# A hybrid of state-space scans, additive attention and graph-routed experts: later PSUM evictions, a softplus step through PSUM, another share of lists and gathers beside the attention, and another order of the last quarters

## The chip, the cores and the metric

The kernel runs on one core of one Trainium2 chip, in one launch. The core has five engines, each with a queue of its own that runs in order: TensorE (PE, with its weight loads as PEld), VectorE (DVE), ScalarE (ACT), GpSimd (POOL) and SyncE (SP, which issues most DMAs). The metric is the device time of one execution in microseconds. Fourteen runs of the kernel before took 15459.08 to 15480.63, with a median of 15470.4.

## The reference, cut to what matters

All data is float32: x is 4 x 32 x 96 x 256, four batches of 3072 tokens with 256 channels.

```python
xn = group_norm(x)
x = x + mamba_d(mamba_t(xn))            # two selective scans, along 96 steps, then along 32
t = x.reshape(4, 3072, 256)
# additive attention, U = 32
q, k = ln(t) @ Wt, ln(t) @ Wx
e = (tanh(q[:, :, None] + k[:, None] + bh) * Wa).sum(-1) + ba
t = t + softmax(e) @ ln(t)
# graph attention over 1048576 edges gives gates; 4 experts, top 2
h = ln(t) @ W_gat                        # 12288 rows
agg = segment_softmax_sum(h, edges)      # scores, exp, sums by destination
w = softmax(top2(mean_heads(ln(agg))))
t = t + sum_e w_e * (gelu(ln(t) @ W1[e] + b1[e]) @ W2[e] + b2[e])
```

Inside a scan block the step size is a softplus, `dt = softplus(dt_w @ dbl + dt_b)`, the state is `h = exp(dt * A) * h + dt * B * u`, and `y = sum(h * C)`. Both ends of the 1048576 edges are drawn from 65536 numbers, while there are 12288 rows: an edge with a destination outside drops out, and a source outside reads the last row. The kernel sorts the edges out itself; those with a source outside are only counted per destination.

## The kernel before, in words

**Order of the work.** For PE, ACT, DVE and POOL the instructions stand in the order in which the program writes them. Two generators are interleaved by hand. `Attention.units` (L779) yields twice per slot: a slot is one column of the attention, that is one tanh over 128 x 3072 on ScalarE (L802, with three buffers `th`). After each yield the other generator, `steps`, adds one half slot of other work. The kernel runs through these stages: the scans of the first batch alone; attention of batches 0 to 2 beside the scans of the next ones; the last attention beside edge lists, early expert products and gathers; and the tail.

**Attention.** Eight slots make a unit of 32 queries, and there are 384 units. In the first half of a slot the tanh is issued, then the other work's first half, then 16 products that reduce the tanh of two slots before into the bank `pe` (L778; one buffer). After the eighth, VectorE takes the maximum of `pe` (L848) and ScalarE the exponential `pr` (L855). The steps that follow are done one per slot, in its second half: four transposes of `pr` on PE into the bank `ptw` and their copy to `pT` on VectorE (`turn`, L862 and L864), two more with their copy, 24 products with the values (L871), and the copy of their sum (L877). All of these use one PSUM buffer in turn (`psum`, one bank). Four units make a tile of 128 queries; its last steps (`tile_tail`: L900 to L937) go on in the same way: the maxima `mx`, a transpose `pm` and its reduction `g`, a second transpose and `f`, an exponential, four small products `sf` on GpSimd (L921), the products `po` with them (L926), and the output with its statistics and its store. A step that returns nothing lets a piece of side work (`beside`) follow in that slot: normalization and keys of the next batch, tables of finished tiles.

**Scans.** `Layer0.run` gives a block of 384 columns 48 slots. `back` fills them with decays on ScalarE (L378, into two PSUM tiles dA), inputs dB (L386), scans (L395, two of 384 columns at a time) on VectorE and products and sums on GpSimd (L402 to L411). `front` prepares the next block in the same slots: at slots 33 to 44 the softplus. For each of four chunks a product fills the bank `pt` (L284), VectorE forms the rectified part and an argument in SBUF (L300, L301), ScalarE takes exp in place (L308), GpSimd adds one (L312), VectorE takes the rounding error of that sum (L316), GpSimd subtracts it (L320); then one Ln over all four (L329), and two additions (L335). These slots are fixed by hand. The first 17 blocks are "lead" blocks with another sharing between the engines. `Beside` uses the bank `ex` of the pool `ps_x` in slots 0 to 30 for some expert products.

**Lists, counts and gathers.** Once the scans are done, `steps` gives each slot `EDGE_US` = 1.9 units of list work (`Edges.sort`, VectorE, each piece with its own estimate in us). The lists end with one-hot products that count edges (L1174, L1188), one pair per slot, as far as PE has room by the planner's account. When the lists have ended, 324 destination gathers (`gd`, L1009, GpSimd) are issued, three per slot. In PE's room `Experts.early` also computes expert units in pairs.

**Tail.** `tail` lays its work out on numbered steps; an expert unit (block of 512 rows, expert) takes three. 37 units are left. The edges come in four quarters of nine parts of 12 columns; part m stands at step `t = G0 + PART * m // 2`: gathers of its rows (L1286, and the destination gathers not done yet) ten steps ahead, scores at t, one-hots (`spread`, L1319 and L1323) and products (`place`, L1333) after. A quarter's `finish` computes the gates of its six blocks. Blocks whose expert outputs are there before their gates are "kept": stored to memory (L1669), fetched again (L1724, four outputs in one transfer) and summed with the gates at steps four apart (L1662). The quarters' order is

```python
QUARTERS = 3, 2, 0, 1
for m in range(4 * PQ):
    j = QUARTERS[m // PQ] * PQ + m % PQ
    t = G0 + PART * m // 2
```

Of the kernel before, what the change touches and what calls it, by code (L numbers as in the profile page):

```python
# [17 lines left out]
F32 = mybir.dt.float32  # L18
# [8 lines left out]
P = 128  # L27
# [34 lines left out]
EDGE_US = 1.9  # L62
G0, PART = 10, 6
QUARTERS = 3, 2, 0, 1
# [10 lines left out]
class Layer0:  # L75
# [96 lines left out]
    def front(self, blk, lead):  # L172
# [107 lines left out]
        def step(e, s_mm, s_out):  # L280
            @at(s_mm)
            def _():
                v["pt"] = ps.tile([P, T], F32, tag="pp", name="pt")
                nc.tensor.matmul(v["pt"], self.wf["dt"][:, e * P:(e + 1) * P], v["dbl"][:DR, :],  # L284
                                 start=True, stop=True)

            ua, ub, dt = (lambda: v["ua"][:, e, :]), (lambda: v["ub"][:, e, :]), (
                lambda: blk["dt"][:, e, :])  # L290

            @at(s_out)
            def _():
                bias = self.wf["dtb"][:, e:e + 1]
                if lead:
                    nc.scalar.activation(dt(), v["pt"], AF.Relu, bias=bias)
                    nc.scalar.activation(ua(), v["pt"], AF.Abs, bias=bias)
                else:

                    nc.vector.tensor_scalar(dt(), v["pt"], bias, 0.0, ALU.add, ALU.max)  # L300
                    nc.vector.scalar_tensor_tensor(ua(), dt(), -2.0, v["pt"], ALU.mult, ALU.add)  # L301

            @at(s_out + 1)
            def _():
                if lead:
                    nc.scalar.activation(ua(), ua(), AF.Exp, scale=-1.0)
                else:
                    nc.scalar.activation(ua(), ua(), AF.Exp, bias=self.wf["dtb"][:, e:e + 1])  # L308

            @at(s_out + 2)  # L310
            def _():
                nc.gpsimd.tensor_scalar(ub(), ua(), 1.0, None, ALU.add)  # L312

            @at(s_out + 3)
            def _():
                nc.vector.scalar_tensor_tensor(ua(), ub(), 1.0, ua(), ALU.subtract, ALU.subtract)  # L316

            @at(s_out + 5)
            def _():
                nc.gpsimd.tensor_tensor(dt(), dt(), ua(), ALU.subtract)  # L320

        step(0, 33, 33)
        step(1, 34, 35)
        step(2, 36, 36)
        step(3, 37, 37)

        @at(41)
# [3 lines left out]
        for e in range(0, EC, 2):  # L331
            @at(44 + e // 2)
# [14 lines left out]
    def back(self, blk, then):  # L347
# [121 lines left out]
        for e in range(EC):  # L469
# [19 lines left out]
            put(12 * e + 4, gate_product(e), 0 if blk["lead"] else 1)  # L489
            put(12 * e + 5, gate_tanh(e))  # L490
            put(12 * e + 6, gate_out(e))
# [140 lines left out]
class Attention:  # L632
# [40 lines left out]

    def psum(self, name):
# [91 lines left out]
    def units(self, side):  # L766
# [24 lines left out]
        while i < B * PER + LAG or todo:  # L791
            b, col = self.entry, self.col = divmod(i, PER)
            if b < B and "krep" not in self.state[b]:

                yield
                yield
# [7 lines left out]
            yield  # L804
            busy = tail = None
# [11 lines left out]
            if tail:  # L817
# [3 lines left out]
                todo = tail()  # L821
            elif todo:
                busy = todo.pop(0)()
# [14 lines left out]
    def unit_tail(self, b, n, pe):  # L838
# [20 lines left out]
        def turn(i0, i1):  # L859
            pt, pr, pT = self.psum("ptw"), v["pr"], v["pT"]  # L860
            for i in range(i0, i1):
                nc.tensor.transpose(pt[:, (i - i0) * P:(i - i0 + 1) * P], pr[:, i * P:(i + 1) * P],  # L862
                                    self.ident)
            nc.vector.tensor_copy(pT[:, i0:i1, :].rearrange("p i x -> p (i x)"),  # L864
                                  pt[:, :(i1 - i0) * P])

        def values():
# [5 lines left out]
            s["pv"] = pv  # L873
            return "pv"

        def kept():
            nc.vector.tensor_copy(pvs[:, u, :], s["pv"][:, :C + 1])  # L877

        first, second = (lambda: turn(0, 4)), (lambda: turn(4, NK))
        first.us, second.us, values.us = 0.7, 0.4, 2.9  # L880
        steps = [first, second, values, kept]
        if u == NU - 1:
            first, *rest = self.tile_tail(b, t, nb, pvs)
            steps = steps[:3] + [lambda: (kept(), first())[1]] + rest
        return weights

    def tile_tail(self, b, t, nb, pvs):
# [10 lines left out]
        def factors():  # L898
            nc.sync.dma_start(x, src)
            nc.vector.tensor_scalar(mx, nb, -1.0, self.ba, ALU.mult, ALU.add)  # L900
            g = self.wk.tile([NU, QU], F32, tag="g", name="g")
# [3 lines left out]
            nc.vector.tensor_reduce(g, pm[:NU, :P].rearrange("p (q r) -> p r q", q=NQT), AX.X,  # L905
                                    ALU.max)
            nc.vector.tensor_copy(g4, g.unsqueeze(1).to_broadcast([NU, NQT, QU]))
            s["g4"] = g4

        def factors2():  # L910
# [3 lines left out]
            nc.vector.tensor_tensor(f, mx, pf[:, :NU], ALU.subtract)  # L914
# [8 lines left out]
        def together():  # L923
# [4 lines left out]
            s["po"] = po  # L928
            return "po"

        def outputs():
            po = s["po"]
# [6 lines left out]
        return [factors, factors2, factors3, spread, together, outputs]  # L939
# [260 lines left out]
class Graph:  # L1200
# [4 lines left out]
    def __init__(self, ctx, tc, a, ed, tab_s, tab_a, gates):  # L1205
# [8 lines left out]
        self.got, self.parts = {}, 4 * CQ // GP  # L1214
# [65 lines left out]
    def gather(self, j):  # L1280
# [4 lines left out]
        for u in range(GP):  # L1285
# [3 lines left out]
            ed.gather(q, c0 + u)  # L1289
        self.got[j] = gs  # L1290

    def scores(self, j):
# [13 lines left out]
        self.v = v  # L1306

    def spread(self, j, g):
# [13 lines left out]
        v = self.v[:, g * GG:(g + 1) * GG, :]  # L1322
# [4 lines left out]
    def place(self, j, g, ol, rh):  # L1327
        nc = self.nc
        c0 = (j * GP + g * GG) % CQ
        if c0 == 0:  # L1330
            self.pa = self.ps.tile([P, JB], F32, tag="pa", name="pa")
        for u in range(GG):
            nc.tensor.matmul(self.pa[:, :NT * ROW], ol[:, u, :],  # L1333
# [3 lines left out]
    def finish(self, q):  # L1337
# [5 lines left out]
        nc.vector.tensor_tensor(acc, acc, self.pa[:, :NT * ROW].rearrange("p (n f) -> p n f", f=ROW),  # L1343
# [331 lines left out]
def tail(tc, a, ed, ex, w, tab_s, tab_a, gates):  # L1675


    with ExitStack() as ctx:
# [14 lines left out]
        for m in range(4 * PQ):  # L1693
            j = QUARTERS[m // PQ] * PQ + m % PQ
# [9 lines left out]
            if m % PQ == PQ - 1:  # L1704
                fin, q = {}, QUARTERS[m // PQ]
# [157 lines left out]
def whole(tc, a, dram, out):  # L1863
# [11 lines left out]
    with ExitStack() as ctx:  # L1875
        actx, lctx, ectx = ExitStack(), ExitStack(), ExitStack()
        with tc.manual_schedule(engines={E.PE, E.Activation, E.DVE, E.Pool}):
# [10 lines left out]
            def steps():  # L1888
# [15 lines left out]
                while True:  # L1904
# [23 lines left out]
                    for _ in range(3 if columns else 0):  # L1928
# [102 lines left out]
```

## Time and profile before

| what | us or share |
|---|---|
| median of 14 runs | 15470.4 |
| the profiled execution, its own time | 15481.81 |
| its span, first to last instruction | 15479.8 |
| ACT busy | 12181.3 (79%) |
| PE busy | 11839.5 (76%) |
| DVE busy | 11078.3 (72%) |
| POOL busy | 8983.7 (58%) |
| tanh of the attention, L802, 3072 of 2.847 | 8666.6 |
| granted TensorE clock, mean | 0.882 |

The profile is one execution. Its page gives each engine's busy share in 40 slices of 387 us, a digit per slice in tenths; "waits" name who waited, at which line, for whom, with total us, times and the longest; groups by line give count, busy us, mean ns, and the idle time just before with what ended it; a timeline gives start and duration. A DMA_INDIRECT on POOL is a gather; L802 means line 802 of the kernel before. Idle time of an engine that does not set the pace costs nothing.

### The profile page before, as it was taken

What the parts mean: (1) busy time and instruction counts of PE and PEld (TensorE: products, weight loads), DVE (VectorE), ACT (ScalarE), POOL (GpSimd) and SP (SyncE); (2) the same over time, 40 slices, a digit from 0 to 9 for tenths busy, and PEclk for the clock granted to TensorE, in tenths of its full rate; (3) what the DMA queues carried; (4) which work ended last, traced back from release to release, by engine and by line L of the source; (5) the groups of instructions that cost most, each with busy time, mean ns of one, the idle gap of its engine ahead of it and who ended that gap; (6) DMA issues with size and microseconds to landing.
All of it is one profiled execution on the core that took longest, in us unless ns stands there. A gap on an engine that the chain in (4) does not pass through costs nothing.

```text
span 15479.8 us, 224265 instructions
## 1 busy us (share of the span) xinstructions
PE 11839.5 (76%) x86496; PEld 5198.1 (34%) x86496; DVE 11078.3 (72%) x15711; ACT 12181.3 (79%) x9326; POOL 8983.7 (58%) x6586
## 2 busy tenths in 40 slices
PE   5666665777777777888888777788877878887897
PEld 2223332222222233333333333333333334443454
DVE  7888888777777787777777877577767783331368
ACT  3444334999999979999999899999998989998221
POOL 4555557777777767777777677577750000007663
PEclk8988886888888878889898888999988989998998
DMA  5666665445444444454444444355541000001224
GB/s 190 206 203 203 196 201 162 144 147 152 148 147 147 151 156 145 148 152 150 147 145 154 153 145 151 112 155 152 151 129 40 23 16 15 10 25 22 52 62 127
DMA packets 1197833, 1986.89 MB, mean 128 GB/s; under 512 B 411984, under 2 KB 645072, under 8 KB 1194320
## 3 DMA queue, kind: packets, MB, share of 16 engines
q1 hardware_dynamic: 1169104, 1967.10, 40.7%
q0 software_dynamic: 27648, 5.36, 0.9%
q8 instruction: 680, 11.14, 0.3%
q14 instruction: 401, 3.28, 0.1%
HBM read 1864.71 MB, written 107.35 MB: 127 GB/s over the span
## 4 chain that ended last, share of the span: by engine, by line
ACT 18%; PE 17%; DVE 9%; POOL 6%; issue 6%; DMA 1%; SPq 0%; DVEq 0%; POOLq 0%; ACTq 0%
ACT th L802 13%; PE pe L778 6%; POOL gd L1009 2%; ACT dA L378 2%; PE pv L871 2%; DVE h L395 2%; PE po L1585 2%; PE pa L1333 2%; PE ph L1577 1%; POOL h L402 1%; ACT pr L855 1%; PE ptw L862 1%; POOL gs L1286 1%; PE ex L1502 1%; DVE dB L386 1%
## 5 line engine op out<-in xcount | busy, mean ns | idle before, releaser
L802 ACT ACTIVATE th<-krep,qsel 128x3072 f32<-128x3072 f32 x3072 | 8666.6, 2847 | 403.5 <-PE pe L778 385.6
L778 PE MATMUL pe<-th,wa_blk 128*32 128x384 f32 x49152 | 5110.4, 544 | 1637.7 <-ACT pr L855 1261.3
L402 POOL TENSOR_TENSOR h<-h,bC 128x768 f32<-128x768 f32 x2048 | 3782.0, 1847 | 2872.5 <-DVE h L395 2636.5
L395 DVE TENSOR_TENSOR_SCAN h<-dA,dB 128x384 f32<-128x384 f32 x4096 | 3681.9, 940 | 818.4 <-ACT dA L378 614.3
L778 PEld LDWEIGHTS pe<-th,wa_blk 128*32 128x32 f32 x49152 | 1472.0, 117 | 4272.8 <-issue 1946.0
L386 DVE TENSOR_TENSOR dB<-bB,dtu 128x768 f32<-128x768 f32 x2048 | 1945.2, 950 | 133.3 <-DMA bB<-bc 89.7
L378 ACT ACTIVATE dA<-dt,t_A 128x380 f32<-128x380 f32 x2048 | 1134.4, 572 | 993.3 <-DVE h L395 987.6
L378 ACT ACTIVATE dA<-dt,d_A 128x372 f32<-128x372 f32 x2048 | 1108.7, 563 | 674.5 <-DVE h L395 667.9
L421 PE MATMUL py<-h,ident 128*128 128x384 f32 x2176 | 990.8, 587 | 693.9 <-POOL h L402 693.0
L921 POOL TENSOR_SCALAR sf<-sel,f 128x32 f32<-128x32 f32 x384 | 153.4, 423 | 2316.3 <-ACT f L917 2196.3
L409 POOL TENSOR_TENSOR h<-h 128x768 f32<-128x768 f32 x752 | 1424.5, 1894 | 46.9
L864 DVE COPY pT<-ptw 128x512 f32<-128x512 f32 (+1 forms) x768 | 425.5, 554 | 1120.5 <-PE ptw L862 1119.5
L871 PE MATMUL pv<-xn,pT 128*32 128x257 f32 x18432 | 1092.4, 385 | 84.3 <-DVE pT L864 82.6
L421 PEld LDWEIGHTS py<-h,ident 128*128 128x128 f32 x2176 | 437.2, 219 | 1252.3 <-POOL h L402 1028.2
L410 POOL TENSOR_TENSOR h<-h 128x384 f32<-128x384 f32 x752 | 798.2, 1061 | 58.9
L411 POOL TENSOR_TENSOR y<-y,h 128x384 f32<-128x384 f32 x752 | 767.7, 1021 | 59.0
L871 PEld LDWEIGHTS pv<-xn,pT 128*32 128x32 f32 x18432 | 585.4, 111 | 633.7 <-DVE pT L864 147.6
L1286 POOL DMA_INDIRECT gs<-tab_s,si x432 | 504.6, 1168 | 265.4 <-issue 122.1
L316 DVE SCALAR_TENSOR_TENSOR uab<-uab 128x384 f32<-128x384 f32 x256 | 390.8, 1527 | 194.3 <-POOL uab L312 190.1
L1659 ACT ACTIVATE h<-ph,b 128x512 f32<-128x512 f32 x148 | 100.4, 687 | 533.5 <-PE ph L1577 533.2
L1009 POOL DMA_INDIRECT gd<-tab_a,di x432 | 428.2, 991 | 133.1 <-issue 133.1
L848 DVE TENSOR_REDUCE nb<-pe 128x1 f32<-128x768 f32 x384 | 361.8, 942 | 196.4 <-PE pe L778 196.2
(292 smaller groups left out, 15395.1 us busy)
## 6 DMA issues: line engine op xcount, KB each, us to landing
bB<-bc SPq DMA_DIRECT2D x2048, 384.0 KB
bC<-bc SPq DMA_DIRECT2D x2048, 384.0 KB
all<-kept SPq DMA_DIRECT2D x19, 2048.0 KB
x<-x SPq DMA_DIRECT2D x144, 256.0 KB
x<-x SPq DMA_DIRECT2D x192, 128.0 KB
xt<-xn2T SPq DMA_DIRECT2D x41, 512.0 KB
kept<-ko SPq DMA_DIRECT2D x39, 512.0 KB
qsel<-xn2T SPq DMA_DIRECT2D x75, 256.0 KB
```

The costliest lines, as they stand in the source:

```text
L378: nc.scalar.activation(inner(dA[:, :T]), inner(blk["dt"][:, e, :]), AF.Exp, scale=blk["w"]["A"][:, e, i + s:i + s + 1])
L386: nc.vector.tensor_tensor(dB, blk["bB"].pop(j), z["dtu"].unsqueeze(1).to_broadcast([P, SB, T]), ALU.mult)
L395: nc.vector.tensor_tensor_scan(h[:, s, :], z.pop(("dA", e, i + s))[:, :T], z["dB"][:, s, :], 0.0, ALU.mult, ALU.add)
L402: nc.gpsimd.tensor_tensor(h, h, blk["bC"].pop(j), ALU.mult)
L409: nc.gpsimd.tensor_tensor(h0, h0, h1, ALU.add)
L410: nc.gpsimd.tensor_tensor(h0[:, 0, :], h0[:, 0, :], h0[:, 1, :], ALU.add)
L411: nc.gpsimd.tensor_tensor(y[e], y[e], h0[:, 0, :], ALU.add)
L421: nc.tensor.matmul(z["py"], self.ident, h[:, s, :], start=(i == 0), stop=(i == DS - 1))
L778: nc.tensor.matmul(pe[q * QU:(q + 1) * QU, j, :KQ // 2], self.wa[:, k, :], th[:, c0:c0 + KQ // 2], start=(k == 0), stop=(k == NK - 1))
L802: nc.scalar.activation(th, s["krep"], AF.Tanh, bias=s["qsel"][:, col:col + 1])
L871: nc.tensor.matmul(pv[q * QU:(q + 1) * QU, :C + 1], pT[:, i, q * QU:(q + 1) * QU], s["xn"][:, q * NK + i, :], start=(i == 0), stop=(i == N ...
L1009: self.nc.gpsimd.indirect_dma_start(out=self.gd[:, q, c, :], out_offset=None, in_=self.tab_a[q].rearrange("p n f -> (p n) f"), in_offset=b ...
```

## The change

Constants: `EDGE_US` 1.9 becomes 2.4, `PART` 6 becomes 5, and `QUARTERS` goes: the quarters come in the order 0, 1, 2, 3. Destination gathers beside the attention: two per slot instead of three. In the tail, each part of quarters 0 to 2 also issues four destination gathers of quarter 3. So that quarters can overlap, `v` and `pa` are kept by part and quarter.

The softplus of blocks that aren't lead: exp goes to the bank `ex`, VectorE does the addition (before: GpSimd) and the subtraction from that bank in one slot, and the four chunks stand two slots apart. GpSimd's subtraction, Ln and the two additions follow; the gate product of the last chunk moves one slot.

The attention: evictions of the small bank are put on a list, `later`, which is worked off in the first half of the next slot, after the other generator's half and before the scores. A tile's first step is split (maxima, then factors), and side work goes ahead of a step instead of after it.

```diff
-EDGE_US = 1.9
-G0, PART = 10, 6
-QUARTERS = 3, 2, 0, 1
+EDGE_US = 2.4
+G0, PART = 10, 5
...
                 else:
-                    nc.scalar.activation(ua(), ua(), AF.Exp, bias=self.wf["dtb"][:, e:e + 1])
+                    v["u"] = self.ps_x.tile([P, 512], F32, tag="ex", name="u")[:, :T]
+                    nc.scalar.activation(v["u"], ua(), AF.Exp, bias=self.wf["dtb"][:, e:e + 1])
...
             @at(s_out + 2)
             def _():
-                nc.gpsimd.tensor_scalar(ub(), ua(), 1.0, None, ALU.add)
-
-            @at(s_out + 3)
-            def _():
-                nc.vector.scalar_tensor_tensor(ua(), ub(), 1.0, ua(), ALU.subtract, ALU.subtract)
-
-            @at(s_out + 5)
+                if lead:
+                    nc.gpsimd.tensor_scalar(ub(), ua(), 1.0, None, ALU.add)
+                else:
+                    nc.vector.tensor_scalar(ub(), v["u"], 1.0, None, ALU.add)
+                    nc.vector.scalar_tensor_tensor(ua(), ub(), 1.0, v["u"], ALU.subtract,
+                                                   ALU.subtract)
...
+            @at(s_out + (5 if lead else 3))
             def _():
                 nc.gpsimd.tensor_tensor(dt(), dt(), ua(), ALU.subtract)
 
-        step(0, 33, 33)
-        step(1, 34, 35)
-        step(2, 36, 36)
-        step(3, 37, 37)
-
-        @at(41)
+        for e, (s_mm, s_out) in enumerate(((33, 33), (34, 35), (36, 36), (37, 37)) if lead else
+                                          ((33, 34), (35, 36), (37, 38), (39, 40))):
+            step(e, s_mm, s_out)
+
+        @at(41 if lead else 43)
...
-            @at(44 + e // 2)
+            @at(44 + e // 2 * (1 if lead else 2))
...
+            g = 12 * e + (5 if e == EC - 1 and not blk["lead"] else 4)
+            put(g, gate_product(e), 0 if blk["lead"] else 1)
+            put(g + 1, gate_tanh(e))
+            put(g + 2, gate_out(e))
...
             yield
+            late, self.later = self.later, []
+            for f in late:
+                f()
             busy = tail = None
...
+            elif todo and hasattr(todo[0], "us"):
+                if not todo[0].full:
+                    beside()
+                todo.pop(0)()
+                busy = True
             elif todo:
-                busy = todo.pop(0)()
+                todo.pop(0)()
...
-            nc.vector.tensor_copy(pT[:, i0:i1, :].rearrange("p i x -> p (i x)"),
-                                  pt[:, :(i1 - i0) * P])
+            self.later.append(lambda: nc.vector.tensor_copy(
+                pT[:, i0:i1, :].rearrange("p i x -> p (i x)"), pt[:, :(i1 - i0) * P]))
...
-            s["pv"] = pv
-            return "pv"
-
-        def kept():
-            nc.vector.tensor_copy(pvs[:, u, :], s["pv"][:, :C + 1])
+            self.later.append(lambda: nc.vector.tensor_copy(pvs[:, u, :], pv[:, :C + 1]))
+
+        steps = [self.step(lambda: turn(0, 4), 0.7), self.step(lambda: turn(4, NK), 0.4),
+                 self.step(values, 2.9, True)]
...
+        for c in range(4 * j, min(4 * j + 4, CQ)):
+            ed.gather(3, c)
...
-            j = QUARTERS[m // PQ] * PQ + m % PQ
+            j = m
...
-                    for _ in range(3 if columns else 0):
+                    for _ in range(2 if columns else 0):
                         ed.gather(*columns.pop(0))
```

The rest of the diff does the same for the tile's last steps: the reduction `g`, the factors `f` and the output with its statistics and store are put on `later`, and the step with the maxima and the load of x stands by itself, put on `later` by the last unit's value products.

## The prediction

> **What bounds the kernel now.** I read the page's 40 slices for the stages, then the busy time by stage, then the waits of ScalarE in each.
>
> ```profile
> PE   5666665777777777888888777788877878887897
> DVE  7888888777777787777777877577767783331368
> ACT  3444334999999979999999899999998989998221
> POOL 4555557777777767777777677577750000007663
> ```
>
> ```profile
> core 0: us, PE busy (x) PEld busy (x) DVE busy (x) ACT busy (x) POOL busy (x), PEclk, DMA share, GB/s
> 2570.00:11533.00 8963.00, 7005.69 (x57369) 2895.90 (x57368) 6794.42 (x9265) 8448.32 (x6290) 6520.75 (x4668) 0.88 0.48 147
> 11533.00:12747.00 1214.00, 920.53 (x8466) 388.56 (x8470) 933.66 (x1490) 1023.57 (x423) 27.80 (x41) 0.89 0.10 31
> 12747.00:13920.00 1173.00, 1037.14 (x11196) 494.48 (x11192) 450.70 (x889) 1142.94 (x469) 24.25 (x57) 0.94 0.04 13
> 13920.00:14350.00 430.00, 325.38 (x2984) 142.26 (x2977) 71.05 (x139) 356.42 (x149) 307.96 (x332) 0.87 0.17 28
> 14350.00:15480.00 1130.00, 945.02 (x2904) 548.78 (x2902) 675.34 (x1237) 228.66 (x285) 626.92 (x546) 0.91 0.32 82
> ```
>
> The rows are the stages: attention beside the scans, lists, one-hot counts, gathers, tail (the scans alone, before 2570, keep their code). ScalarE, with its tanh of 2.85 us per slot, sets the pace until 14350: 94% busy in the first row, 97% in the third. So up to there a gain is a ScalarE wait that goes. In the tail it is PE, 84% busy.
>
> **Beside the scans (2570 to 11856).** ScalarE's waits here, the most this stage can give:
>
> ```profile
> ACT dA L378 <- DVE h L395: 305.5, 355, 7.4
> ACT th L802 <- PE pe L778: 218.1, 212, 5.6
> ACT pr L855 <- DVE nb L848: 55.2, 48, 13.7
> ```
>
> VectorE waits far longer (633.1 us for ptw at L864, 152.1 for pt at L300), but only what reaches ScalarE counts. For each gap of over 0.3 us before a dA I looked, in the trace, for VectorE's longest stall from 5 us before the gap on: 40.6 us of gaps stand behind uab L316, 27.9 behind dt L300, 22.2 behind g L905, 73 behind qsel, hb and xTc (not changed), 84.8 behind a busy VectorE, 0.3 behind the pT copy. So the long ptw wait is mostly slack, and deferring that copy gives almost nothing here.
>
> ```profile
> L316 DVE SCALAR_TENSOR_TENSOR uab<-uab 128x384 f32<-128x384 f32 x180 | 295.6, 1643 | 94.0 <-POOL uab L312 89.8
> L301 DVE SCALAR_TENSOR_TENSOR uab<-dt,pt 128x384 f32<-128x384 f32 x180 | 99.7, 554 | 6.2
> ```
>
> The same operation takes 1.64 us with both inputs in SBUF beside GpSimd's work, 0.55 us with one in PSUM. After, VectorE does the addition (like L300, 0.61 us) and the subtraction (like L301, 0.55): 1.16 for 1.64, times 184: 88 us less, and GpSimd loses 184 x 1.24 us. The steps now start in slots 34, 36, 38, 40, one PSUM bank each in turn, so the waits for pt and for GpSimd's sum go. I count the three named gaps (91 us) and half of the busy ones (42). The exp into PSUM I price like dA (0.56 for 0.60 us, 6 us in all): nothing. Its bank, ex, is free from slot 31 on, and each exp comes a slot after the subtraction that empties the bank; one that waited would hold the tanh behind it. The sums of dt (L335) end in slot 46 and the last gate in 43; they are read from slot 48 on, so the two slots more are covered. The eight added table loads are in the tail, where ScalarE is idle.
>
> [...]
>
> What it adds: each eviction now stands behind the next slot's scans (two of 0.94 us). The second pT copy starts 4.2 to 4.9 us (medians by batch) into a slot of 3.7 to 4.1, some 0.3 to 0.8 into the next one; behind the scans it ends near 2.5. The value products wait for it. They start at 2.1 to 2.9 now and take 2.8; the scores queued behind them on PE end at 2.7 to 3.7 of their slot, and the tanh after needs their buffer by 3.7 to 4.1. I take 0.1 us for each of 277 units, 30 us; the ends are nothing and 0.9 us (250), the room that the fastest of these batches has. Behind a late tanh all of ScalarE's queue is late, the decays too. Sum: -91 - 42 + 30, about **-100**; ends -220 (all busy gaps and a fifth of the waits for pe go too) and +120 (0.9 us per unit).
>
> The tile's own last steps (L900 to L935) each move by half a slot; the load of x and the store to x2 go with them on SP. That store waits there for x (873 us in all, 61 times), with loads of bB and bC queued behind, for which VectorE waits 89.7 us; store and x move together, so the wait is no longer: nothing. PE's wait of pm for mx (87.5 us) goes; that is in the gaps behind g.
>
> **Lists.** By the starts of the tanh, 346 slots take 1233 us (3.56 each).
>
> ```profile
> ACT th L802 <- PE pe L778: 119.3, 91, 8.1
> ACT pr L855 <- DVE nb L848: 69.1, 20, 13.7
> ```
>
> VectorE is busy 934 us of 1214 and waits for most of the rest, so it is full. A slot takes 2.4 units of lists for 1.9: laying the program out gives 274 slots, then 72 more at the counting stage's 2.99 us. VectorE's work left in the 274 is 934 less 72 slots of attention at 0.31 and two expert pairs at 8.7 (eight L1616, four L1628), 895 us or 3.27 a slot; that is the lower end, with all its waits gone. The upper is today's slot with 0.5 us more, 4.07. I take 3.6, near today's row: 274 x 3.6 + 72 x 2.99 + two pairs' gelu (13) = 1214: **-20** (-110 to +110).
>
> **Counting.** Both orders have about 385 slots at 2.99, with 28 us of ScalarE waits. The deferred copies stand behind a one-hot that itself waits for PE (L1174, 177.8 us): **+10** (-28 to +40).
>
> **Gathers beside attention.**
>
> ```profile
> L1009 POOL DMA_INDIRECT gd<-tab_a,di x320 | 303.9, 950 | 97.1 <-issue 97.1
> ```
>
> Each costs 0.95 + 0.30 = 1.25 us, so three per slot are 3.76 us: 108 slots take 397 us, 3.68 each, GpSimd's pace. It reaches ScalarE through sf: PE's waits for sf are 58.9 us in three places, up to 23.0, and th then waits 71.4. At two per slot GpSimd needs 2.5 us, under the 2.99, over 162 slots that end at slot 737 of 768. The last 118 slots fall from 435 us to 118 x 3.05 (2.99, and the gelu of two expert pairs, as today): **-75** (-50 to -90).
>
> **Tail.** Both orders have 37 expert units of three steps. From the timeline a unit is 16 products of 0.43 us and 32 of 0.226 on PE, 14.1 us; a part's placing is 24 of 0.403, 9.7 us. Before: a part each three steps, 23.8 us, and the trace has 23 to 24 late on; but the first nine parts (quarter 3, 24 gathers each) come 30 us apart (14472 to 14742), on GpSimd. After: 2.5 steps, 11.75 + 9.7 = 21.4 us on PE; 16 gathers at 1.45 (24 took 35) are 23.2. GpSimd starts at 14390 and the first placing is at 14472, its first 16 gathers are done by about 14415, so it has some 50 us in hand, and loses 27 x 1.8 = 49. So PE leads: 14472 + 35 x 21.4 = 15221, three gate computations inside the stretch at 12 us (36 for 23.5 in the trace), 15257, and 14 steps of units alone at 4.7: 15323. What follows:
>
> ```profile
> 15398.14 0.65 DVE L1343 TENSOR_TENSOR acc<-acc,pa 128x480 f32<-128x480 f32 x1
> ...
> 15417.95 0.26 DVE L1402 TENSOR_TENSOR gates<-gates,tot 128x96 f32<-128x96 f32 x1
> 15418.24 15.76 DVE L1662 SCALAR_TENSOR_TENSOR y<-all,gates,y 128x256 f32<-128x256 f32 x32
> ```
>
> Now the last quarter's gates (20 us) and six blocks' sums (62 us to the end) follow PE's last product. After, quarter 3's gates are ready at step 107, beside the units; the six blocks remain: 15385. **-95** (-120 to 0). Twenty more stores and five more fetches on SP, 20 MB, hide under DMA queues that are 32% busy; without that cover, at the 184 GB/s of the last 140 us, 110 us.
>
> [...]
>
> **The sum.** -100 - 20 + 10 - 75 - 95 = -280. The profiled execution took 15481.8 (span 15479.8); the median is 15470.4, 11.4 less. 15481.8 - 280 - 11.4 = **15190**.
>
> **Rivals.** (1) Beside the scans the freed gaps only become others: ScalarE waits for PE and VectorE in turn at each unit's end. For it: the ptw waits are mostly slack. Against: L316's stall has a price of its own. -180: 15290. (2) The tail doesn't do what it says: GpSimd at 1.5 us a gather and the added 20 MB hold PE, and 95 is lost: 15285. (3) Slower: a deferred copy holds the value products, the scores behind them miss their slot, and the tanh waits once per unit, 277 + 98 times. It decides from 280 / 375 = 0.75 us each; at 1.2 us it is +450 - 280: 15640. For it: PE is 83% busy there, and the scores end within 1 us of their limit. Against: PE has slack later in each unit.
>
> **Chances.** Forecast 0.62, (1) 0.18, (2) 0.08, (3) 0.12. A measurement of this kernel can tell about 0.2%, 31 us, from no change. From the first three 0.03, from (3) 0.02 fall within that: faster 0.85, same 0.05, slower 0.10. The range, 15040 to 15410, takes in the first three with the scan stage's two ends, or the lists' two; (3) and both at once stay out.
>
> **What would show it.** Right: the subtraction near 0.55 us, ScalarE's wait for h near 170 us, slots of 3.0 beside the gathers and no wait for sf, parts 21 to 24 us apart from the first on, no gates after PE's last product. Wrong: th waiting for pe well over 218 us beside the scans, list slots over 4, or PE idle between parts.

## The result and the profile after

| | median us | lowest to highest | runs |
|---|---|---|---|
| before | 15472.29 | 15459.08 to 15481.36 | 28 |
| after | 15298.03 | 15289.88 to 15312.79 | 6 |

The ratio is 0.9888, 95% interval 0.9879 to 0.9898: 174 us less, where 280 were forecast (15190; the range of 15040 to 15410 holds the result). The profiled execution after took 15288.94 us, its span 15287.2, against 15479.8.

The 40 slices after, to be laid beside those of before:

```profile
PE   5666764767777767888888777888876878888997
DVE  7888888778777787777777877577768864331467
ACT  3444334999999979999999899999997889999422
POOL 4565556777777767767767677477650000026584
```

ScalarE's run of nines is as long as before, with a dip to 7 and 8 where the lists are denser (VectorE's two eights below it). The tail's slices (the last three) show PE at 9, 9, 7.

The windows of the stages after (columns as in the prediction's table: length, busy time of each engine, clock, DMA share, GB/s); the rows are the scans, lists, counting, gathers, tail:

```profile
2567.00:11406.00 8839.00, 6883.44 (x57312) 2856.61 (x57316) 6710.89 (x9442) 8430.28 (x6290) 6261.97 (x4489) 0.89 0.48 149
11406.00:12468.00 1062.00, 744.85 (x6864) 304.00 (x6860) 913.60 (x1467) 827.56 (x341) 22.75 (x33) 0.89 0.11 32
12468.00:13626.00 1158.00, 1028.05 (x11012) 482.36 (x11008) 432.29 (x838) 1118.48 (x457) 22.52 (x50) 0.94 0.04 12
13626.00:14227.00 601.00, 511.31 (x4823) 217.77 (x4816) 110.81 (x216) 576.68 (x241) 315.28 (x347) 0.93 0.15 29
14227.00:15287.00 1060.00, 937.63 (x2910) 544.72 (x2908) 680.13 (x1239) 240.84 (x295) 655.44 (x546) 0.94 0.40 108
```

In the first row ScalarE is 95% busy (94 before), in the tail PE 88% (84 before). In the lists VectorE is 86% busy (77 before) and ScalarE 78% (84 before): there the bound has gone over to VectorE.

The stages end at different slots in the two kernels, so I compare them between the same starts of the tanh, where (b,s) is slot s of batch b. Profiled executions, us; "to (2,685)" counts from the span's start, the tail from the last tanh to the end:

| | to (2,685) | (2,685) to (3,263) | (3,263) to (3,649) | last 118 slots | tail |
|---|---|---|---|---|---|
| before | 11527.7 | 1233.1 | 1154.9 | 434.7 | 1129.4 |
| after | 11403.4 | 1276.8 | 1174.9 | 371.9 | 1060.2 |
| measured | -124 | +44 | +20 | -63 | -69 |
| forecast | -100 | -20 | +10 | -75 | -95 |

ScalarE's waits beside the scans, 2567 to 11754:

```profile
ACT th L814 <- PE pe L787: 233.8, 248, 4.7
ACT dA L384 <- DVE h L401: 153.7, 160, 7.4
ACT pr L875 <- DVE nb L868: 83.1, 37, 15.5
ACT f L946 <- DVE f L943: 25.6, 21, 3.5
```

The wait for the scans h has halved (305.5 to 153.7), the next two are 16 and 28 us longer, and the last is new: the exponential of a tile's factors f waits for their eviction, which now stands on `later`. The subtraction of the softplus, now with one input in PSUM (minimum, median, maximum in ns):

```profile
L316 DVE SCALAR_TENSOR_TENSOR uab<-uab,u x184: 553/554/556, 2470.4 to 11176.8; 128x384 f32<-128x384 f32 x184
```

The lists, waits of ScalarE and then of PE, 11406 to 12468:

```profile
ACT th L814 <- PE pe L787: 134.4, 89, 7.5
ACT pr L875 <- DVE nb L868: 87.2, 24, 15.5
```

```profile
PE pe L787 <- ACT pr L875: 175.6, 30, 20.4
```

This is a chain: the maximum nb of a finished unit stands on VectorE behind list work, pr waits for it up to 15.5 us, and PE's next scores wait up to 20.4 for the bank `pe`, which pr has to read first. Though the window is 152 us shorter than before's, both ScalarE waits have grown (119.3 and 69.1 before).

Beside the gathers, 13626 to 14227, PE's waits:

```profile
PE pe L787 <- ACT pr L875: 80.7, 23, 11.2
PE pe L787 <- ACT th L814: 4.8, 4, 1.5
```

The 58.9 us of waits for GpSimd's sf are gone. In the tail, two stretches of parts (same columns as the windows):

```profile
14271.00:14554.00 283.00, 278.94 (x870) 164.63 (x869) 144.23 (x215) 73.21 (x91) 219.53 (x186) 1.00 0.33 79
14554.00:14946.00 392.00, 359.12 (x1030) 203.50 (x1029) 269.02 (x494) 87.92 (x111) 313.69 (x258) 0.94 0.39 96
```

In the first, PE is 99% busy, and the first ten placings are 20.8 us apart in the mean. In the second it is GpSimd that is full: 258 instructions with 0.3 us between them are 313.7 + 77 = 391 of 392 us. PE waits there for one-hots that stand behind the gathered rows, and the placings are 24 to 25 us apart:

```profile
PE pa L1364 <- DVE rh L1354: 25.2, 7, 7.1
```

### The profile page after: what moved, and what is told of

The parts are those of the page before. It is cut to its first block, busy times and chain, and to the rows that moved or that the text cites. A ratio compares the mean times of both kernels' runs of the same rounds, so it can differ in the third digit from the quotient of the medians.

```text
span 15287.2 us, 224326 instructions
## 1 busy us (share of the span) xinstructions
PE 11718.1 (77%) x86496; PEld 5132.5 (34%) x86496; DVE 10995.2 (72%) x15895; ACT 12174.4 (80%) x9333; POOL 8747.4 (57%) x6402
## 3 DMA queue, kind: packets, MB, share of 16 engines
q8 instruction: 680, 11.14, 0.3%
q14 instruction: 401, 3.28, 0.1%
## 5 line engine op out<-in xcount | busy, mean ns | idle before, releaser
L787 PE MATMUL pe<-th,wa_blk 128*32 128x384 f32 x49152 | 5037.0, 539 | 1668.0 <-ACT pr L875 1445.6
L893 DVE COPY pvs<-pv 128x257 f32<-128x257 f32 x384 | 160.6, 418 | 586.2 <-PE pv L891 585.0
L882 PE MATMUL ptw<-ident,pr 128*128 128x128 f32 x2304 | 475.7, 324 | 114.5 <-DVE pT L884 44.7
```

The source lines that it names most:

```text
L787: nc.tensor.matmul(pe[q * QU:(q + 1) * QU, j, :KQ // 2], self.wa[:, k, :], th[:, c0:c0 + KQ // 2], start=(k == 0), stop=(k == NK - 1))
```

## The experiments

Twelve runs in four sets, each set beside the kernel before (e1 to e4, e5 to e8, e9 to e11, e12; the expectations say "call" for a set). The expectations name theories by letters. **A**: the parts add; the scan stage's gain is the softplus's, the lists' loss comes of their density. **B**: the deferred evictions give the scan stage's gain. **C**: the deferral costs the lists' time. **D**: in the third batch, the softplus slots fall badly on the attention's units. **E**: the lists lose at the units' ends, where nb waits. **F** came last: GpSimd's gathers hold up the instruction fetches.

In the second to fourth set the kernel before took 370 to 390 us more, and the changed kernel's profile there (e9) shows 369 us more where the destination gathers run. So these sets are read by the ratio to the kernel before in the same set and by stages that end before that stretch; e12 goes into it.

### Each part alone, on the kernel before

e1_softplus, the softplus blocks only:

```diff
-                    nc.scalar.activation(ua(), ua(), AF.Exp, bias=self.wf["dtb"][:, e:e + 1])
+                    v["u"] = self.ps_x.tile([P, 512], F32, tag="ex", name="u")[:, :T]
+                    nc.scalar.activation(v["u"], ua(), AF.Exp, bias=self.wf["dtb"][:, e:e + 1])
```

with the addition, the subtraction and the slots as in the change.

> Only the softplus part on the kernel before (exp to PSUM, the sum on VectorE, chunks two slots apart). Theory A (the scan stage's 122 us come from this part; the deferral gives nothing there): the stage up to the last scan shortens by 90 to 120 us, total near 15365. Theory B (the deferred evictions gave them, by taking away VectorE's waits for PE): total within 30 us of 15472.

e2_later, the attention's list `later` only:

```diff
-            nc.vector.tensor_copy(pT[:, i0:i1, :].rearrange("p i x -> p (i x)"),
-                                  pt[:, :(i1 - i0) * P])
+            self.later.append(lambda: nc.vector.tensor_copy(
+                pT[:, i0:i1, :].rearrange("p i x -> p (i x)"), pt[:, :(i1 - i0) * P]))
```

with the other evictions and the split step as in the change.

> Only the deferred evictions on the kernel before. Theory A: within 30 us of 15472 beside the scans, and the lists not slower than 1233 us for their 346 slots. Theory B: the scan stage shortens by about 110 us, total near 15360. Theory C (the lists' loss of 44 us comes from copies that stand behind list work): the same 346 slots take 1250 us or more, total 15490 or more unless B holds too.

e3_lists:

```diff
-EDGE_US = 1.9
+EDGE_US = 2.4
...
-                    for _ in range(3 if columns else 0):
+                    for _ in range(2 if columns else 0):
```

> Only the denser lists (2.4 units per slot) and two gathers per slot on the kernel before. Theory A (VectorE is full, so density alone costs): the 346 slots from the first list on take 40 us more than 1233, the last 118 slots 60 us less, total near 15450. Theory C: the 346 slots take 1210 us or less, total near 15385.

e4_tail:

```diff
-G0, PART = 10, 6
-QUARTERS = 3, 2, 0, 1
+G0, PART = 10, 5
...
+        for c in range(4 * j, min(4 * j + 4, CQ)):
+            ed.gather(3, c)
```

> Only the tail's part (quarters 0 to 3 in order, a part each 2.5 steps, quarter 3's gathers four per part) on the kernel before. Theory A (the parts add up): the tail shortens by about 70 us, total near 15400. Rival (the tail gained only because GpSimd came into it without a backlog of gathers): 30 us or less, total 15440 or more.

Measured beside a kernel before at 15477.98 us:

| | median us | ratio, 95% interval | to (2,685) | (2,685) to (3,263) | (3,263) to (3,649) | last 118 | tail |
|---|---|---|---|---|---|---|---|
| e1 | 15439.56 | 0.9973 [0.9961, 0.9986] | 11487.3 | 1231.4 | 1156.8 | 434.3 | 1128.8 |
| e2 | 15403.54 | 0.9948 [0.9932, 0.9965] | 11487.2 | 1184.5 | 1169.9 | 423.1 | 1133.4 |
| e3 | 15504.53 | 1.0016 [1.0007, 1.0026] | 11534.8 | 1313.5 | 1169.2 | 370.6 | 1129.6 |
| e4 | 15403.35 | 0.9951 [0.9934, 0.9967] | 11515.5 | 1232.5 | 1162.6 | 434.1 | 1058.3 |

The medians give -38, -74, +27 and -75, together -160 for -174: the parts nearly add, as A has it. But the scan stage's gain is not the softplus's alone, nor the deferral's, so neither A nor B holds there: each of e1 and e2 takes 40 us off the way to (2,685), both together 124 (stages that a kernel doesn't touch scatter by some 12 us, as e4's first column shows). Split at (2,0), where the third batch begins, the way is:

| | to (2,0) | (2,0) to (2,685) |
|---|---|---|
| before | 8821.3 | 2706.3 |
| e1 | 8722.3 | 2765.0 |
| e2 | 8767.9 | 2719.3 |
| after | 8699.5 | 2703.9 |

So the softplus alone gives 99 us in the first two batches and loses 59 in the third; with the deferral that loss is gone. And the deferral takes 49 us off the lists, so C falls with the wrong sign. e4's tail is 71 us shorter although its gathers beside the attention are as before, so the rival of e4 falls.

Waits of ScalarE beside the scans, of e1 and then of e2, 2567 to 11840:

```profile
ACT dA L385 <- DVE h L402: 222.2, 259, 7.4
ACT th L810 <- PE pe L786: 217.3, 236, 5.2
ACT pr L863 <- DVE nb L856: 106.6, 35, 17.3
```

```profile
ACT th L807 <- PE pe L780: 253.7, 221, 6.7
ACT dA L378 <- DVE h L395: 203.8, 291, 7.4
ACT pr L868 <- DVE nb L861: 50.3, 46, 13.5
ACT f L939 <- DVE f L936: 30.7, 25, 3.2
```

Of the 305.5 us that ScalarE waited for h, the softplus alone takes 83, the deferral alone 102. e1 pays 51 of it back in waits for nb; these fall in its third batch. The deferral costs 36 us of waits for pe, the price which the third rival put at up to 450, and 31 us of waits for f, which are not there before.

e3 is the clean test of the density. In the lists it loses 80 us, twice what was expected, and in the last 118 slots it gets 64 back. Its waits in the lists, 11533 to 12747:

```profile
ACT th L802 <- PE pe L778: 142.5, 108, 9.8
ACT pr L855 <- DVE nb L848: 121.1, 29, 16.2
```

### Two cures that did nothing, and the tail's gathers

All three are edits of the changed kernel, as are those that follow. e7_phase moves the softplus slots of the third batch by one, away from the units' ends:

```diff
+        o = int(not lead and (b, way) == (B - 1, "d"))
...
-            step(e, s_mm, s_out)
+            step(e, s_mm + o, s_out + o)
```

(the steps after them likewise).

> The changed kernel with the softplus slots of the last batch's second scans one slot later, so that the doubled VectorE work stands in slots 2, 4, 6 and 0 of the units of eight instead of 1, 3, 5 and 7. Theory D (the softplus part lost 59 us in the third batch because its doubled work falls on the slot where a unit ends): the third batch's 685 slots take 25 to 50 us less than 2704, total near 15260. Rival (the loss has another cause): within 10 us of 15298.

The median was 15703.64 us, 0.9905 [0.9889, 0.9922] of a kernel before at 15853.09. Slots (2,0) to (2,685) took 2722.9 us, for 2704 to 2712 in the changed kernel and its other variants up to then, and ScalarE's waits for h there were 25.0 us for 22.0. D falls; e1's loss in this batch goes away with the deferral, and what causes it stays open.

e8_unit_ends does no list work in the slots where a unit ends, and 8/7 as much in the others:

```diff
-                    us_v = min(us_v, 0.0) + EDGE_US
-                    while lists
+                    ends = att.col % 8 == 1
+                    us_v = us_v if ends else min(us_v, 0.0) + EDGE_US * 8 / 7
+                    while not ends and lists
```

> The changed kernel with no list work in the slot where a unit ends, and 2.74 units in the seven others. Theory E (density costs through the maximum that stands behind list work at a unit's end, with the exponential on ScalarE waiting for it): ScalarE's wait for the maximum falls from 87 us in the lists to under 30, the 346 slots take 1220 us or less, total near 15240. Theory A (VectorE is simply full): 1277 us and 15298 within 15.

The median was 15691.08 us, 0.9894 [0.9878, 0.9911]. The wait of pr for nb in the lists fell from 87.2 to 66.8 us, the wait of th for pe rose from 134.4 to 158.3, and the lists took 1295.2 us for 1276.8 to 1286.0. E falls, and the total stays, as A has it: with the list work taken out of the unit's end the time is lost elsewhere.

e6_no_q3_gathers leaves the fourth quarter's 108 destination gathers out of the tail (that part of the destinations is filled with zeros):

```diff
-            ed.gather(q, c0 + u)
-
-        for c in range(4 * j, min(4 * j + 4, CQ)):
-            ed.gather(3, c)
+            if q < 3:
+                ed.gather(q, c0 + u)
```

> The changed kernel without quarter 3's 108 destination gathers in the tail (its destination terms are set to zero, so that part of the computation is left out). Theory A (GpSimd's gathers set the tail's pace, 23.0 us a part where PE needs 21.4): parts 21.5 to 22 us apart, the tail some 40 us shorter, total near 15255. Rival (VectorE or PE sets it): parts stay 23 us apart, total within 15 us of 15298.

The median was 15653.20 us, 0.9866 [0.9847, 0.9884]. In the profiles the tail took 1045.3 us, for 1073.8 and 1074.5 in e7 and e8 beside it: with these gathers it is some 29 us longer, 12 of them before the first placing and 17 between the placings. GpSimd took 21.6 us per part for 24.7 in e7, and the placings of the first 26 parts came 21.7 us apart for 22.2. GpSimd's gathers stayed 84 to 106 us ahead of their placing throughout, so PE led.

The size holds for these later sets. There, the changed kernel's first placing in the tail (e9) comes 157 us after the last tanh instead of 116, and PE stands once for 28.2 us with no releaser that the profile shows. In that time GpSimd gets 113 us ahead of the placings instead of 72, and the 35 parts take 783 us for 807. So in the first profile these gathers may hold up the parts by more: 807 less e6's 766 is 41 us, an estimate.

### How dense should the lists be?

e5_thin_lists and e10_thin_again are one kernel, the change without its third part; e11_mid_lists lies between; e9_after_again is the changed kernel itself.

```diff
-EDGE_US = 2.4
+EDGE_US = 1.9
...
-                    for _ in range(2 if columns else 0):
+                    for _ in range(3 if columns else 0):
```

e11 has only `EDGE_US = 2.2`.

e5:

> The changed kernel with the lists and gathers as before (1.9 units, three gathers per slot). Theory A (the parts add up; this part alone cost 27 us): about 15250, 50 us under the changed kernel, with 1185 us for the 346 slots of the lists. Rival (denser lists pay together with the deferral): 15300 or more.

e9:

> The changed kernel once more, unaltered, as the measure for the two kernels beside it: the second call's chip was 2.4% slower for every kernel, so e5 is compared with the changed kernel on one chip here. Both theories: 0.989 of the kernel before, as on record (15298 of 15472), and the stage table of its first profile within 15 us a row where this chip runs the stretch beside the destination gathers like the first one.

e10:

> The same edit as e5_thin_lists: the changed kernel with the lists back at 1.9 us a slot and three destination gathers a slot, so the softplus, deferral and tail parts alone. Theory A (the parts add; e1, e2 and e4 alone gave -38, -74 and -75, e3 alone +27): 15472 - 187 = 15285 to 15298 - 27 = 15271, so 13 to 27 us less than the changed kernel; e5's own ratio of 0.9844 says 15231, 67 less. By stages: lists from slot (2,685) to (3,263) about 1192 for 1277, counting 1164 for 1175, the last 118 slots 434 for 372. Rival (e5's lead came from that chip alone, the denser gathers cost what the denser lists save): within 15 us of the changed kernel, with the lists still 85 shorter.

e11:

> The changed kernel with list work of 2.2 us a slot for 2.4, the gathers still two a slot. The lists end about 24 slots later, at (3,600), and the gathers by (3,761), just inside attention. If density costs in proportion (85 us between 1.9 and 2.4): lists 51 us of 85 dearer than thin ones, 34 less than in the changed kernel, the gathers as there (3.16 us a slot), so 15264, and with two gathers a slot kept this is the fastest of the three. If the loss sets in where VectorE has no room left (steep at the end): most of the 85 goes, 50 to 70 less, 15230 to 15250. Rival (the loss is already whole at a density a little above 1.9): within 15 us of the changed kernel, slower than the thin one.

| | list units a slot | median us | ratio, 95% interval | (2,685) to (3,263) | from (3,263) to the last tanh |
|---|---|---|---|---|---|
| e5 | 1.9 | 15607.73 | 0.9844 [0.9828, 0.9861] | 1191.6 | 1928.1 |
| e10 | 1.9 | 15613.62 | 0.9845 [0.9831, 0.9858] | 1191.7 | 1933.7 |
| e11 | 2.2 | 15646.54 | 0.9866 [0.9851, 0.9881] | 1240.2 | 1917.1 |
| e9 | 2.4 | 15685.10 | 0.9894 [0.9879, 0.9909] | 1286.0 | 1915.7 |

(The kernel before: 15853.09 beside e5, 15858.81 beside the others.) The thin lists win twice, by 71 us in the second of these sets; that is more than e10's Theory A had (13 to 27), and its rival falls. e11 is not the fastest of the three, as its expectation had it, but it lies in the middle: at three fifths of the added density its lists show 48.5 of the 94.3 us, where proportion gives 57. So most of the loss is not at the dense end.

The period of the 274 slots from (2,685) on says why: 3.41 us at 1.9 units, 3.88 at 2.4. So a list slot takes its units plus some 1.5 us (1.4 in e11, 1.6 without the deferral). That remainder is not all attention: VectorE's evictions and maxima for the attention are 0.31 us a slot, and side work, waits and list pieces that take other than their estimates are in it too, not separated. A slot without lists takes ScalarE's 2.98 (the mean of the 72 after the lists in the changed kernel's first profile; its tanh there takes 2.85). The lists' work is the same in both kernels (346 x 1.9 = 274 x 2.4 = 657 units); denser lists put it into 72 fewer slots, and these then take 2.98 in place of the 1.5 saved: 72 x 1.48 = 107 us more, an estimate; 80 (e3) to 94 (e9 against e10) were measured.

In the conditions of the first set the thin version was not run. From there, e2's 2777.5 us from (2,685) to the last tanh against the changed kernel's 2823.6 makes it 46 us faster, near 15250, an estimate; the gains of e1, e2 and e4 added up give 15285. In the later sets it is the fastest version of the study that computes the whole reference.

### The gathers beside the attention

e12_no_gathers:

```diff
-        if (q, c) not in self.have:
+        if q == 3 and (q, c) not in self.have:
```

> The changed kernel without the 324 destination gathers of the first three quarters (that part of the destinations is filled with zeros), everything else as it is; the 108 gathers of the fourth quarter stay in the tail. In the later calls every kernel, the one before too, spent about 370 us more where these gathers run, and in the trace the instruction fetches of the core fall silent for as long as a run of gathers lasts (none between 13863.8 and 13937.6 us in e9, beside 64 gathers from 13851.5 to 13931.9; every 10 to 20 us in the changed kernel's first profile). Theory F (the gathers hold up the fetches, and the stalled slots are engines without instructions): the 191 slots from (3,576) to the end go at 2.95 to 3.0 us each, about 567 us, whichever way this call runs, for 602 in the first profile and 971 in e9; with a kernel before at about 15470 the time is 35 less than 15298, with one at 15860 it is 400 less than e9, 15260 to 15290 in both. Rival (something else of the later calls slows that stretch, the last attention itself or its loads): beside a kernel before at 15860 the slots stay above 3.5 us. By the way it gives the whole price of two gathers a slot in a call that runs like the first one: the forecast's and Theory A's 3.15 less 2.97, 0.18 us a slot or 35 us.

It took 15328.66 us, 0.9673 [0.9660, 0.9687] of a kernel before at 15847.01. The stretch from (3,576) to the last tanh took 601.9 us, 3.15 a slot; 602.0 in the changed kernel's first profile, with the gathers; 970.9 in e9. The windows of that stretch, e12 and then e9:

```profile
13634.00:14235.00 601.00, 511.37 (x4827) 218.38 (x4820) 110.65 (x216) 576.69 (x241) 8.16 (x24) 0.93 0.09 28
```

```profile
13637.00:14609.00 972.00, 584.13 (x4849) 237.71 (x4846) 111.70 (x218) 579.70 (x241) 317.89 (x348) 0.77 0.09 18
```

Beside the row of 13626 to 14227 above, e12's PE and ScalarE are the same to 0.1 us, and only GpSimd's work has gone, from 315 us to 8. So in the first profile two gathers a slot cost nothing at all, and in the later sets they cost 370 us; the rival (something else in that stretch) falls. In e9 ScalarE and VectorE do the same work as in e12 to 3 us, and PE is busy 73 us longer at a granted clock of 0.77 for 0.93: most of the 370 us is engines that stand still.

The slots did not go at 2.95 to 3.0 us, as the expectation had it, and the time was not in its 15260 to 15290. My 0.18 us a slot was wrong: 3.15 is the attention's own pace there, with PE's 80.7 and 80.6 us of waits for pr. And the tail, whose own gathers are still there, took 1079.1 us for 1060.2, with its first placing 159 us after the last tanh for 116.

## Why the prediction was right, and where it was off

The range holds the result, but the forecast itself missed it by 108 us. The stages give 88 of these (24 more gained beside the scans; 64, 10, 12 and 26 lost in the others); the rest is how far the two profiled executions lay from their medians. By the number alone rivals (1) and (2), at 15290 and 15285, were nearer than 15190, yet the stages show neither: (1) has nothing gained beside the scans, where 124 were measured, and (2) nothing in the tail, where 69 were. Most of the miss is in the lists, for which no rival stood.

**The scan stage, -100 for -124.** The price of the operands was right: 0.554 us for the subtraction with one input in PSUM, 0.550 for the addition, and the exp into PSUM 0.566. The 1.64 us before was a mean of two kinds:

```profile
L316 DVE SCALAR_TENSOR_TENSOR uab<-uab x256: 525/1972/2215, 93.5 to 11292.8; 128x384 f32<-128x384 f32 x128
```

Of the 184 in blocks that aren't lead, 56 took 0.53 to 0.69 us and 111 took 2.03 to 2.22; the three that no GpSimd instruction overlapped took 0.55. So L316 with both operands in SBUF was not slow by itself, only beside some of GpSimd's work: the 85 that mostly overlapped its sums (L409) have a median of 2.16, four times the 0.55 of those that nothing overlapped. After, with one input in PSUM, all 184 took 0.553 to 0.556 us. What in GpSimd's work makes the difference, no run separates.

The failed step is the one after it: "I looked, in the trace, for VectorE's longest stall from 5 us before the gap on", and from it "0.3 behind the pT copy" and "deferring that copy gives almost nothing here". e2, which moves the other evictions too, shows 40 us here and 49 in the lists. With 12 us of looking back on the same trace, the pT copy stands behind 43.8 us of ScalarE's gaps, dt 40.4, uab 40.6, and the "busy VectorE" is left with some 20 of its 84.8. A slot takes 4 us; a stall can leave VectorE behind for two or three slots, and what I called a busy VectorE would be its backlog. That reading is argued, not shown: the 12 us were chosen afterwards, and with 8 us the pT copy has 8.1, with 16 it has 31.4. What is shown is that the deferral gains. The sum came out near by luck: "half of the busy ones" (42) and the 30 of cost stood in the place of a gain that the prediction had put at nothing.

**The lists, -20 for +44.** Mis-sized: 3.6 us a slot against 3.88. "I take 3.6, near today's row" chose the row of 3.56 at 1.9 units, though the prediction itself had said that VectorE is full. Where VectorE is full, 0.5 units more cost 0.5 us: e3 shows 4.01 us a slot for 3.52 before, near the upper end of 4.07. The deferral, which takes 49 us off this stage, hid more than half of e3's loss of 80; it also shows that VectorE was not quite full, for e2 does the same list work in less time.

**Counting, +10 for +20**: within its bounds. **Gathers, -75 for -63**: the mechanism held (no wait for sf, GpSimd no longer the pace); 3.05 was taken for the slot; 3.15 is what it takes with the gathers and, as e12 shows, without them.

**The tail, -95 for -69.** From the first to the last placing 35 parts took 807 us for the forecast's 785, and from there to the end 138 for 128. "some 50 us in hand" and "16 gathers at 1.45" were the terms: they took 24.4 us per part, 1.53 each, so GpSimd lost 3.7 us a part on PE's 20.8 instead of 1.8. Its lead over the placings fell from 72 us at the first part to 37 at the tenth and stayed at 30 to 41 up to the twenty-ninth; over those parts GpSimd, not PE, set the pace. e6 confirms that these gathers cost time, though in conditions where GpSimd starts with more in hand. That is a part of the second rival, at a quarter of its price; whether the added 20 MB have a share in it no run separates. The quarter gates do lie beside the units: VectorE's end of the program has only the blocks' sums in it.

```profile
15225.97 3.99 DVE L1693 SCALAR_TENSOR_TENSOR y<-all,gates,y 128x256 f32<-128x256 f32 x8
15234.30 2.44 DVE L1693 SCALAR_TENSOR_TENSOR y<-all,gates,y 128x256 f32<-128x256 f32 x5 [4.34 <-DMA y<-x]
...
15273.57 7.92 DVE L1693 SCALAR_TENSOR_TENSOR y<-all,gates,y 128x256 f32<-128x256 f32 x16 [3.37 <-DMA y<-x]
```

PE's last product ends at 15223.2, 64 us before the end; before it was 82, with the last quarter's gates in them.

**The rivals.** The first (freed gaps become others) came true in part: of the 152 us less that ScalarE waits for h, 16 came back in waits for pe, 28 for nb and 26 for f. The third (one missed tanh per unit) did not: the deferral alone added 36 us of waits for pe and 31 for f.

## To carry to other kernels

Before side work is packed more densely, write down what a slot costs with it and without it: here its units plus 1.5 us with lists against 2.98 without, so that each slot freed of lists cost more than it saved, and thin lists are better. When gaps of one engine are traced to another, try several lengths of looking back, do not book "it was busy" as a cause, and let a run decide. And run each part of a change alone: the sum here hid a part that made the kernel slower.

## What the runs showed of the hardware

In three of the four sets the gathers beside the attention cost about 370 us (from (3,576) to the last tanh 970.9 us in e9, 601.9 in e12 without them); in the changed kernel's first profile they cost nothing (602.0). The instruction fetches are the DMA transfers of the kind "instruction": in that first profile 680 packets with 11.14 MB on q8 and 401 with 3.28 MB on q14, 16 and 8 KB each. In e9 they pause beside the gathers, for 73.8 us in the run below. The DMA view of one run of 64 gathers, first the changed kernel's first profile (13854 to 13934; queue, kind: packets, MB, share), then e9 (13852 to 13932):

```profile
q0 software_dynamic: 1970, 0.13, 9.9%
q1 hardware_dynamic: 1632, 2.10, 8.3%
q8 instruction: 5, 0.08, 0.4%
```

```profile
q0 software_dynamic: 2016, 0.13, 9.5%
q1 hardware_dynamic: 560, 0.79, 3.3%
q8 instruction: 1, 0.02, 0.1%
q14 instruction: 1, 0.01, 0.0%
```

The gathers are the same, but e9 has two fetches for five, at 13852.9 and 13926.7 us (the expectation of e12 has these times 10.9 us too late). Meanwhile the engines mostly stand still; ScalarE's, then PE's timeline there:

```profile
13875.56 2.85 ACT L814 ACTIVATE th<-krep,qsel 128x3072 f32<-128x3072 f32 x1 [12.73 <-remote]
13925.98 2.85 ACT L814 ACTIVATE th<-krep,qsel 128x3072 f32<-128x3072 f32 x1 [47.56 <-remote]
```

```profile
13893.70 0.59 PE L891 MATMUL pv<-xn,pT 128*32 128x257 f32 x1 [2.21 <-issue]
13896.50 0.59 PE L891 MATMUL pv<-xn,pT 128*32 128x257 f32 x1 [2.21 <-issue]
13899.30 0.59 PE L891 MATMUL pv<-xn,pT 128*32 128x257 f32 x1 [2.21 <-issue]
```

Two tanh lie 50 us apart, and PE does one matmul every 2.80 us, with no releaser that the profile shows ("remote", "issue"). With the gathers out, e12 takes 3.15 us a slot beside a kernel before that is as slow as in the other late sets. So it is shown that the gathers cause the stalls. That they do it by holding up the fetches, Theory F, is not shown: both profiles have 47 fetch packets from (3,576) to the last tanh, so a program that stands still for another reason would fetch as rarely; PE goes on, slowly, while nothing is fetched; and the tanh at 13925.98 starts ahead of the fetch at 13926.7. Why it happens in some sets and not in others is open as well: of two sets on the same chip one showed it and one did not, and the kernel before was the same program. How the gathers bring about e9's stalls, up to 50 us for one slot, no run here tells.
